# Reordering the queues of a two-layer graph kernel: table steps, gathers, roots and matrix products

## The chip, the cores and the metric

The kernel runs on one core of one Trainium2 chip. The metric is the device time of one execution in microseconds (us). The kernel before has a median of 2475.27 us over three runs (2471.58, 2475.27, 2481.45). A separate execution, taken by the hardware profiler, is the source of every duration below.

The core has five instruction queues: TensorE (PE, matrix products; its weight loads are PEld), VectorE (DVE), ScalarE (ACT), GpSimd (POOL) and SyncE (SP, which here only starts transfers). Each works through its own queue in the order in which the program wrote it, and semaphores hold an instruction until what it needs is done.

## The reference, cut to what matters

```python
# B, C, N = 32, 512, 1024; adj is 512 x 512, all in float32
def layer0(x):
    q, k = einsum('c,bcn->bn', wq, x), einsum('c,bcn->bn', wk, x)
    s = leaky_relu(q[:, None, :] + k[:, :, None], 0.01)
    att = softmax(s, axis=-1)                         # over n, for each m
    agg = einsum('bcn,bmn->bcm', x, att)
    return relu(einsum('oc,bcm->bom', adj, agg) + bm[None, :, None])
def layer1(x):
    return einsum('bnf,nm->bmf', x, adj * adj) + bias
x = layernorm(x + layer0(x))                          # over the last axis, eps 1e-5
x = layernorm(x + layer1(x))
```

## The kernel before, in words

The N x N attention matrix is never made. The score is q[n] + k[m], and leaky ReLU has one slope on each side of zero. So for a given m the softmax over n splits into the n whose q is above -k[m] and those below. With the nodes sorted by q, each side is a prefix or a suffix sum. One batch b goes through these steps:

* `project(b, nt, part)` (L256): four x tiles times [wq, adj^T, wk], giving for each of 8 node tiles (nt) a PSUM tile `zp`, which ACT copies (L264) into `zrow`: q, 512 products, k.
* `peak` (L271) and `spread` (L278 to L302): PE transposes q into every partition (`qb`), and through `mx` (L282) the largest q. DVE takes it as `qmax`, `bw` (L285, L286), saves k as `kc` and overwrites k in `zrow` by 1 (L297, L298). ACT copies `qb` (L293) into `lq`.
* `place` (L315, L319): DVE counts, for each of 8 node tiles, how many q are larger: the ranks. `send` (L324): an indirect DMA, started by POOL, scatters 128 rows of `zrow` to the table `td` in DRAM in rank order. `count` (L343): ACT counts signs of q + k, and `share` (L351 to L361) turns the counts into the rows to gather.
* `fetch` (L371, L376): SP reads the sorted rows back into `zs`, in 9 blocks for the prefix and the suffix.
* `weigh` (L390 to L406): ACT makes exponentials of the sorted q, DVE multiplies them into triangular matrices `lq`.
* `table(b, step)` for step 0 to 8 (L418 to L434): PE multiplies triangles and sorted rows (`tp`), two blocks a step; ACT copies the result (`ts`, L423); the last running sum of each block is carried to the next one, one row by POOL (L427) and one by ACT (L429); SP stores `ts` to `td` in two transfers (L432). Step n+1 on PE needs both carried rows of step n. Step 8 carries none.
* `pick` (L439): an indirect DMA by POOL gathers, for each of 8 node tiles, prefix, suffix and own row (128 rows of 6168 bytes). `shares` (`own` and `norm`, L458 to L472), `scale` (ACT, L485) and `gain` (DVE, L493, two instructions a tile) mix the three rows.
* `turn(b, ot)`: PE transposes the mixture back (`op`, L531), ACT adds bm and applies ReLU (L535). `join`: DVE adds x (L542) and takes mean and variance (`stats`, L502, L504). `root`: POOL computes (variance + eps)^-0.5 (L510, L511). `shift` (DVE, L517) and `apply` (ACT, L523, or DVE, L525) normalise.
* `layer1(b)`: the 1024-wide product with adj * adj, in a Strassen-like form with 7 half-size products (A11, S1, S2, S3, S4, A22, A12; L576, two halves m each) of sums T1 to T4 (`sums`, L559: DVE, or POOL for T2 to T4 with a = 1). DVE reads the products out of PSUM (`read`, L586, 18 reads).
* `stats1`, `shift`, `apply`, `store` normalise the second layer's result `v` and write it out (L622).

The order is written out by hand (`tc.manual_schedule()`): each engine's queue holds its instructions in the order of the calls. The steady part is `slot(s)` for s = 1 to 29, which works on four batches at once: `new` = s+2 is projected, tables are made for `mid` = s+1, batch s goes through gains, turns, joins and layer 1, and `old` = s-1 is normalised and stored. The first part of a slot is a loop of z = 0 to 7 over the projections; from z = 4 on, each z carries two table steps and one turn. A POOL queue of z = 4 therefore reads: roots of `old` 0 and 1, carried row of step 0, carried row of step 1, root of y 0. After the loop come `peak`, the sums T2 to T4 with a = 0, `spread`, and `phase`: table step 8, then the 14 half products with ranks, scatters and gathers threaded between. In it POOL issues the sums T2 to T4 with a = 1, scatters 0 to 2, gathers 0 to 5, scatters 3 and 4, gather 6, scatters 5 to 7, gather 7; SP then starts the fetch of `new`.

`ps_mm` has three PSUM buffers that projections, turns, products and some table steps take in turn, `ps_t` has one, for `qb` and the other table steps. `begin`, `opening` and `end` handle the batches at the two ends, where fewer are in flight.

Of the kernel before, what the change touches and what calls it, by code (L numbers as in the profile page):

```python
# [23 lines left out]
def gat_gcn_resnorm_kernel(  # L24
# [46 lines left out]
    nc = tc.nc  # L71
# [196 lines left out]
    def peak(b):  # L268

        tops[b] = small.tile([P, 1], F32, name=f"q8_{b}", tag="q8")  # L270
        nc.vector.tensor_reduce(tops[b], zrow[:, :, 0], AX.X, ALU.max)  # L271

    def spread(b, to="lq"):
# [13 lines left out]
        if to == "v":  # L287
            qs = vpool.tile([P, N], F32, name=f"qs_{b}", tag="v")
            nc.scalar.copy(qs, qb)
            qb = qs  # L290
        elif to == "lq":
            qs = lq[:, 0:N]
            nc.scalar.copy(qs, qb)  # L293
        else:
            qs = qb
        kc = small.tile([P, NT], F32, name=f"kc_{b}", tag="kc")
        nc.vector.tensor_copy(kc, zrow[:, :, C + 1])  # L297
        nc.vector.memset(zrow[:, :, C + 1], 1.0)  # L298
# [7 lines left out]
        info[b] = (qs, kc, sgn, qmax)  # L306
# [254 lines left out]
    def layer1(b):  # L561
# [10 lines left out]
        def make(w, y, m):  # L572
            if m == 0 or b == B - 1:
                ops[b, w] = ps_mm.tile([P, 2, H], F32, name=f"o{w}_{b}_{m}", tag="mm")
            for a in range(CT // 2):
                nc.tensor.matmul(  # L576
                    ops[b, w][:, m, :], quarters[w][:, a, m * P : (m + 1) * P], part(y, a),
                    start=(a == 0), stop=(a == CT // 2 - 1),
                )
# [9 lines left out]
        for w, y in (  # L589
            ("A11", "Y11"), ("S1", "T1"), ("S2", "T2"), ("S3", "T3"),  # L590
            ("S4", "Y22"), ("A22", "T4"), ("A12", "Y21"),
        ):
            for m in range(2):
                mul.append(lambda w=w, y=y, m=m: make(w, y, m))
        for m in range(2):
            u, v = m, 2 + m
            for name, what in (
# [5 lines left out]
                ("12", (u, hi, "S4", m, u, hi)),  # L603
                ("22", (v, hi, None, m, v, lo)),
                ("21", (v, lo, "A22", m, v, lo)),
                ("11", (u, lo, "A12", m, u, lo)),
# [10 lines left out]
    def stats1(b, mt):  # L617
        stats((1, b, mt), vs[b, mt])
        root(1, b, mt)
# [4 lines left out]
    def rest(b, after):  # L624

        mul, get, reads = layer1(b)
        names = (("c1",), ("c5",), ("u2",), ("u3", "u4"), ("12", "22"), ("21",), ("11",))
        sums(b, ("T1", 0), ("T1", 1), ("T2", 0), ("T3", 0), ("T4", 0))
        for i in range(len(mul)):
            mul[i]()  # L630
            if i == 3:
                sums(b, ("T2", 1), ("T3", 1), ("T4", 1))
            for name in names[i // 2]:
                if b == B - 1:
                    get[name, i % 2]()
                elif i % 2:
                    reads(name)
            after(i)

    def last(b, late):  # L640

        halves = []

        def after(i):
            mt = 1
            if i == 0:
                late(b - 1)
            if i == 11:
                for mt in (2, 3):
                    stats1(b, mt)  # L650
                mt = 1
                st = small.tile([P, NH, 6], F32, name=f"st_1_{b}_{mt}", tag="st")
                nc.vector.bn_stats(st[:, 1, :], vs[b, mt][:, hi])
                halves.append(st)
                for mt in (2, 3):
                    shift(1, b, mt)
                    apply(1, b, mt)
                    store(b, mt)

            if i == 12:  # L660
                stats1(b, 0)
                shift(1, b, 0)
                apply(1, b, 0)
                store(b, 0)

        rest(b, after)
        t, st = vs[b, 1], halves[0]
        nc.vector.bn_stats(st[:, 0, :], t[:, lo])
        mv = small.tile([P, 2], F32, name=f"mv_1_{b}_1", tag="mv")
        nc.vector.bn_aggr(mv, st)  # L670
        due[1, b, 1] = [t, mv]
        root(1, b, 1)
        shift(1, b, 1)
        t, mv, rs, nb = due.pop((1, b, 1))
        nc.scalar.activation(t[:, lo], t[:, lo], AF.Identity, bias=nb, scale=rs)
        nc.vector.tensor_scalar(t[:, hi], t[:, hi], rs, nb, ALU.mult, ALU.add)
        for some in (lo, hi):
            nc.sync.dma_start(out=out[b, P : 2 * P, some], in_=t[:, some])

    def phase(s, mid, new, step=None, done=0):  # L680
# [3 lines left out]
        def rank(*some):  # L684
            for nt in some:
                if nt >= done:
                    place(new, nt)
                    if not done:
                        count(new, nt)
                if nt < 3:  # L690
                    send(new, nt)

        if step is not None:
            table(mid, step, pool=ps_mm)
        mul[0]()
        mul[1]()
        sums(s, ("T2", 1), ("T3", 1), ("T4", 1))
        rank(0, 1, 2)
        mul[2]()
        mul[3]()  # L700
        get["c1", 0]()
        rank(3)
        get["c1", 1]()
        rank(4, 5)
        for mt in range(5):
            pick(mid, mt)
        reads("c5")
        mul[4]()
        mul[5]()
        pick(mid, 5)  # L710
        rank(6)
        get["u2", 0]()
        rank(7)
        get["u2", 1]()
        send(new, 3)
        send(new, 4)
        mul[6]()
        mul[7]()
        pick(mid, 6)
        for nt in range(5, NT):  # L720
            send(new, nt)
        reads("u3", "u4")
        mul[8]()
        mul[9]()
        reads("12", "22")
        mul[10]()
        mul[11]()
        pick(mid, 7)
        fetch(new)
# [4 lines left out]
        scale(mid, range(NT // 2))  # L734
        reads("11")
        gain(mid, range(NT // 2))

    def begin():
# [24 lines left out]
        for z in range(NT):  # L763
# [14 lines left out]
            if z == NT // 2 - 1:  # L778
                fetch(1)
# [3 lines left out]
            if z == NT - 4:  # L783
                weigh(1, 0)
            if z == NT - 3:
                table(1, 0)
                for mt in range(NT):
                    pick(0, mt)
                weigh(1, 1)
            if z == NT - 2:  # L790
                table(1, 1, nc.vector)
        table(1, 2, nc.vector)
        peak(2)
        spread(2, "ps")

    def opening():

        for nt in range(NT // 2):
            place(2, nt)
            table(1, 3 + nt, pool=ps_mm)  # L800
        share(1)
        shares(0, 0, NT // 2)
        scale(0, range(NT // 2))
        count(2, 0)
        table(1, 7, pool=ps_mm)
        count(2, 1)
        gain(0, range(NT // 2))
        shares(0, NT // 2, NT)
        scale(0, range(NT // 2, NT))
        table(1, 8, pool=ps_mm)  # L810
        gain(0, range(NT // 2, NT))
        for nt in range(2, NT):
            count(2, nt)
        for ot in range(CT):
            turn(0, ot)
            join(0, ot)
            root(0, 0, ot)
            load(3, ot)
        shift(0, 0, CT - 1)
        apply(0, 0, CT - 1)  # L820
        sums(0, ("T1", 0), ("T1", 1), ("T2", 0), ("T3", 0), ("T4", 0))
        phase(0, 1, 2, done=NT // 2)

    def slot(s):
# [4 lines left out]
        for z in range(NT):  # L829
# [5 lines left out]
            if step >= 0:  # L835
                table(mid, step)
            if z == NT - 1:
                join(s, CT - 1)
                root(0, s, CT - 1)
# [13 lines left out]
            if z == 3:  # L853
                for mt in (0, 1):
                    stats1(old, mt)
# [6 lines left out]
            if 0 <= ot < CT - 1:  # L862
                join(s, ot)
                root(0, s, ot)
# [5 lines left out]
            if ot == 1:  # L870
                for mt in (2, 3):
                    stats1(old, mt)
# [3 lines left out]
            if new + 1 < B and z >= tz:  # L876
                load(new + 1, ot)
        peak(new)
        shift(0, s, CT - 1)
        sums(s, ("T2", 0), ("T3", 0), ("T4", 0))  # L880
        spread(new)
# [4 lines left out]
        phase(s, mid, new, NB - 1)  # L886

    def end():
# [4 lines left out]
        gain(s, range(NT // 2, NT))  # L893
        weigh(mid, 0)
        for ot in range(CT):
            turn(s, ot)
            table(mid, ot)
            if ot == 1:
                weigh(mid, 1)
            join(s, ot)  # L900
            root(0, s, ot)
            if ot == 1:
                for mt in (0, 1):
                    stats1(old, mt)
            if ot == 2:
                for mt in (0, 1):
                    shift(1, old, mt)
                    apply(1, old, mt, by=nc.vector)
                    store(old, mt)
        shift(0, s, CT - 1)  # L910
        apply(0, s, CT - 1)

        def late(b):
            for mt in (2, 3):
                stats1(b, mt)
            for mt in (2, 3):
                shift(1, b, mt)
                apply(1, b, mt, by=nc.vector)
                store(b, mt)

        def after(i):
            if CT + i < NB:
                table(mid, CT + i)
            if i == 0:
                late(old)
                share(mid)
# [3 lines left out]
            if i in (7, 11):  # L930
                pick(mid, 6 + (i - 7) // 4)

        rest(s, after)
        shares(mid, 0, NT // 2)
        scale(mid, range(NT // 2))
        gain(mid, (0, 1))
        own(mid, NT // 2, NT)
        gain(mid, (2, 3))
        norm(mid, NT // 2, NT)
        scale(mid, range(NT // 2, NT))  # L940
        gain(mid, range(NT // 2, NT))
        for ot in range(CT):
            turn(mid, ot)
            join(mid, ot)
            root(0, mid, ot)
            if ot == 1:
                for mt in (0, 1):
                    stats1(s, mt)
            if ot == 2:
                for mt in (0, 1):  # L950
                    shift(1, s, mt)
                    apply(1, s, mt, by=nc.vector)
                    store(s, mt)
        shift(0, mid, CT - 1)
        apply(0, mid, CT - 1)
        last(mid, late)
# [35 lines left out]
```

## Time and profile before

| | |
|---|---|
| median of three runs | 2475.27 us |
| the profiled execution's own time | 2456.85 us |
| its span, from first to last instruction | 2455.1 us |
| PE busy | 2229.5 us |
| DVE busy | 2005.8 us |
| ACT busy | 1393.3 us |
| POOL busy | 1082.7 us |
| DMA, moved | 548.72 MB, mean 223 GB/s |
| mean granted TensorE clock | 0.965 |
| `qb` of slot 1 to `qb` of slot 29 (28 periods) | 252.68 to 2266.89 us, 71.94 each |
| first product of `phase(0)`, first projection of slot 1 | 172.57, 204.33 us |
| last product of `phase(29)` ends | about 2293.9 us |

The span divides in three: about 204 us of opening, 29 slots, and about 161 us of end. A number such as "[2.03 <-POOL zs L427]" behind an instruction is the idle time of its engine before it, and what released it. Idle time counts only on the engine that sets the pace.

### The profile page before, as it was taken

To read this page: it belongs to the slowest core of one execution; us is meant where nothing else is said; L and a number is where in the kernel's file an instruction comes from. 1 tells how busy PE (TensorE), PEld (TensorE's weight loads), DVE (VectorE), ACT (ScalarE), POOL (GpSimd) and SP (SyncE) were. 2 spreads that over 40 slices of the span, in tenths; PEclk is the share of its full clock that TensorE was granted. 3 is DMA by queue.
4 is the path that set the end of the run, shared out by engine and by line. 5 is a ranking of instruction groups with operands and counts; after the bars stand their busy time and mean duration, and the time that the engine had idled before them with its cause. 6 is when DMAs were issued, how large, how long until landed. Compare 5 with 4: busy or idle time off the path is not lost.

```text
span 2455.1 us, 31484 instructions
## 1 busy us (share of the span) xinstructions
PE 2229.5 (91%) x9520; PEld 1405.4 (57%) x9520; DVE 2005.8 (82%) x4197; ACT 1393.3 (57%) x2176; POOL 1082.7 (44%) x1385
## 2 busy tenths in 40 slices
PE   7858999999999999999999999999999999999665
PEld 6625665566656556655656665565666565566232
DVE  4258888888888888888888888888888888888856
ACT  2553566665556666555666555666655565665521
POOL 1224445444444544444554444455444445543422
PEclk9969999999999999999999999999999999999877
DMA  6546786667777666776766777777677776666631
GB/s 228 152 168 226 232 265 240 218 216 232 255 230 266 238 218 217 235 252 230 259 226 216 226 244 247 238 254 232 208 233 241 240 250 240 220 215 199 225 141 69
DMA packets 176842, 548.72 MB, mean 223 GB/s; under 512 B 26304, under 2 KB 26304, under 8 KB 176672
## 3 DMA queue, kind: packets, MB, share of 16 engines
q1 hardware_dynamic: 117600, 276.65, 38.1%
q0 software_dynamic: 57344, 269.52, 29.1%
q8 instruction: 76, 1.25, 0.2%
q14 instruction: 94, 0.77, 0.1%
q10 hardware_dynamic: 1728, 0.53, 0.1%
HBM read 338.17 MB, written 208.43 MB: 223 GB/s over the span
## 4 chain that ended last, share of the span: by engine, by line
DVE 42%; DMA 15%; PE 13%; issue 8%; POOL 8%; ACT 6%; SPq 0%; DVEq 0%; POOLq 0%; ACTq 0%
DMA rows<-td,idx 13%; DVE st L502 8%; DVE lt L315 8%; DVE v L586 8%; DVE rows L493 7%; PE tp L418 5%; PE zp L256 4%; DVE y L542 3%; POOL rs L511 3%; PE oS L576 2%; DVE rows L559 2%; POOL zs L427 2%; DMA td<-ts 2%; ACT y L535 2%; POOL rs L510 2%
## 5 line engine op out<-in xcount | busy, mean ns | idle before, releaser
L256 PE MATMUL zp<-wmT,x 128*128 128x257 f32 x4096 | 959.4, 387 | 2.9 <-ACT zrow L264 2.9
L256 PEld LDWEIGHTS zp<-wmT,x 128*128 128x128 f32 x4096 | 771.7, 193 | 163.7 <-issue 47.2
L418 PE MATMUL tp<-zs,lq 128*64 128x257 f32 x2304 | 331.9, 406 | 135.3 <-POOL zs L427 118.5
L510 POOL TENSOR_SCALAR rs<-mv 128x1 f32<-128x1 f32 x256 | 74.8, 292 | 759.0 <-DVE mv L504 630.5
L493 DVE SCALAR_TENSOR_TENSOR rows<-rows,ra 128x512 f32<-128x512 f32 x512 | 370.7, 751 | 35.9 <-ACT rows L485 26.8
L423 ACT COPY ts<-tp 128x514 f32<-128x514 f32 x288 | 168.5, 585 | 290.7 <-PE tp L418 249.7
L324 POOL DMA_INDIRECT td<-zrow,ranki x256 | 272.4, 1064 | 119.4 <-DVE ranki L319 54.4
L427 POOL COPY zs<-ts 1x513 f32<-1x513 f32 x254 | 183.5, 722 | 313.2 <-ACT ts L423 313.0
L418 PEld LDWEIGHTS tp<-zs,lq 128*64 128x64 f32 x2304 | 149.6, 140 | 286.2 <-POOL zs L427 168.0
L315 DVE SCALAR_TENSOR_TENSOR lt<-qb,zrow,first 128x1024 int8<-128x1024 f32 x240 | 305.9, 1275 | 1.6
L439 POOL DMA_INDIRECT rows<-td,idx x256 | 263.9, 1031 | 87.3 <-issue 68.7
L461 ACT ACTIVATE ac<-s 128x4 f32<-128x4 f32 x64 | 13.3, 208 | 498.5 <-DVE s L460 498.5
L343 ACT ACTIVATE sg<-lq,kc 128x1024 int8<-128x1024 f32 x232 | 266.3, 1148 | 6.6
L576 PE MATMUL oA<-y,adj_sb 128*128 128x512 f32 x512 | 242.3, 616 | 11.1 <-ACT y L523 11.1
L576 PE MATMUL oS<-rows,ws 128*128 128x512 f32 x512 | 231.7, 604 | 9.7 <-DVE v L586 5.4
L542 DVE TENSOR_TENSOR y<-y,x 128x1024 f32<-128x1024 f32 x128 | 160.8, 1256 | 84.7 <-ACT y L535 84.7
L485 ACT ACTIVATE rows<-rows,ra 128x512 f32<-128x512 f32 x256 | 167.2, 713 | 57.6 <-DVE ra L472 57.6
L264 ACT COPY zrow<-zp 128x514 f32<-128x514 f32 x256 | 147.9, 578 | 89.4 <-PE zp L256 77.7
L531 PE MATMUL op<-ident,rows 128*128 128x128 f32 x1024 | 151.4, 291 | 37.0 <-DVE rows L493 34.3
L511 POOL TENSOR_TENSOR rs<-rs,mhalf 128x1 f32<-128x1 f32 x256 | 172.0, 672 | 21.4
L576 PEld LDWEIGHTS oS<-rows,ws 128*128 128x128 f32 x512 | 97.8, 193 | 138.2 <-issue 128.5
L576 PEld LDWEIGHTS oA<-y,adj_sb 128*128 128x128 f32 x512 | 96.7, 194 | 135.3 <-issue 113.6
(108 smaller groups left out, 2813.3 us busy)
## 6 DMA issues: line engine op xcount, KB each, us to landing
x<-in_x_dram SPq DMA_DIRECT2D x128, 512.0 KB, 4.7
out_dram<-v SPq DMA_DIRECT2D x127, 512.0 KB, 2.7
td<-ts SPq DMA_DIRECT2D x512, 120.5 KB, 2.2
zs<-td SPq DMA_DIRECT2D x64, 602.3 KB, 6.7
zs<-td SPq DMA_DIRECT2D x64, 240.9 KB, 3.3
zs<-td SPq DMA_DIRECT2D x96, 120.5 KB, 3.5
td<-ts SPq DMA_DIRECT2D x64, 96.4 KB, 2.0
td<-zs SPq DMA_DIRECT2D x8, 514.0 KB, 9.1
```

Of the source, the lines that this page charges most:

```text
L256: nc.tensor.matmul(zp[:, h, 0:CE], xb[ct][:, nt * P : (nt + 1) * P], wmT[:, ct, h * CE : (h + 1) * CE], start=(ct == 0), stop=(ct == CT - 1),)
L315: nc.vector.scalar_tensor_tensor(lt, qs, zrow[:, nt, 0:1], first[:, o : o + N], ALU.subtract, ALU.is_lt, accum_out=rank[:, nt : nt + 1],)
L324: sc = nc.gpsimd.indirect_dma_start(out=td[:, :], out_offset=bass.IndirectOffsetOnAxis(ap=ranki[:, nt : nt + 1], axis=0), in_=zrow[:, nt, ...
L343: nc.scalar.activation(sg, qs, AF.Sign, bias=kc[:, nt : nt + 1], accum_out=sgn[:, nt : nt + 1])
L418: nc.tensor.matmul(tp[i * G : (i + 1) * G, h, 0:CE], lw[:, ks[i], :], zs[:, j, h * CE : (h + 1) * CE], start=True, stop=True,)
L427: by.tensor_copy(zs[0:1, to, 1:ZW], ts[0:1, 1:ZW])
L439: nc.gpsimd.indirect_dma_start(out=rows[:, mt, :], out_offset=None, in_=tds[b].rearrange("(s u) c -> s (u c)", u=3), in_offset=bass.Indire ...
L493: nc.vector.scalar_tensor_tensor(u, g[:, k, i, 1 : C + 1], ra[:, k, i : i + 1], u, ALU.mult, ALU.add)
L502: nc.vector.bn_stats(st[:, h, :], t[:, h * H : (h + 1) * H])
L511: nc.gpsimd.tensor_tensor(rs, rs, mhalf, ALU.pow)
L542: nc.vector.tensor_tensor(t, t, xs[b][ot], ALU.add)
L576: nc.tensor.matmul(ops[b, w][:, m, :], quarters[w][:, a, m * P : (m + 1) * P], part(y, a), start=(a == 0), stop=(a == CT // 2 - 1),)
```

## The change

* `peak` now also saves `kc` and writes the ones; before, `spread` did. `spread` always copies `qb` to `lq` (or to `v`).
* In `slot`: root of y 0, 1 and 2 moves from behind its `join` to behind the first table step of the next z; the roots of `old` follow the first table step of z = 4 and z = 6 (`roots`, split from `stats1`). The root of y 3 comes after the loop, behind the carried row of step 7. After the loop the order is `peak`, `spread`, table step 8, and then the normalisations of y 3 and of `old` 2 and 3; before, it was the sums, `spread`, the normalisations, and step 8.
* In `phase`: the sums T2 to T4 with a = 0 (DVE) move in between the ranks. POOL issues two sums, gathers 0 and 1, the third sum, then scatter 0, gather 2, scatter 1, gather 3, scatter 2, gathers 4 and 5, scatter 3, gather 6, scatters 4 and 5, gather 7, scatters 6 and 7. A22 comes before S4, with the reads in the order 22, 21, 12, 11; the gains of tiles 0 and 1 stand before the reads of A12.
* `begin` makes no table of batch 1, and issues the gathers of batch 0 earlier; `opening` makes the 9 table steps of batch 1 between the gains, turns and joins of batch 0, and `phase(0)` is now the same as all others.
* `end`: steps 0 and 1 of the last table stand between gains; T1 is taken before the last join; the old batch's normalisation is applied by ACT in `rest`; the last batch's v 0 and v 1 are normalised and stored by halves.

The diff, cut to its core:

```diff
 def peak(b):
     nc.vector.tensor_reduce(tops[b], zrow[:, :, 0], AX.X, ALU.max)
+    nc.vector.tensor_copy(kc, zrow[:, :, C + 1])
+    nc.vector.memset(zrow[:, :, C + 1], 1.0)
...
 def make(w, y, m):
-    if m == 0 or b == B - 1:
+    if m == 0 or b == B - 1 and w in ("S4", "A12"):
...
-            ("S4", "Y22"), ("A22", "T4"), ("A12", "Y21"),
+            ("A22", "T4"), ("S4", "Y22"), ("A12", "Y21"),
...
+    def ready(b, *some):
+        for mt in some:
+            shift(1, b, mt)
+        for mt in some:
+            apply(1, b, mt)
+            store(b, mt)
...
 def rest(b, after):
-    names = (("c1",), ("c5",), ("u2",), ("u3", "u4"), ("12", "22"), ("21",), ("11",))
-    sums(b, ("T1", 0), ("T1", 1), ("T2", 0), ("T3", 0), ("T4", 0))
+    names = (("c1",), ("c5",), ("u2",), ("u3", "u4", "22"), ("21",), ("12",), ("11",))
     for i in range(len(mul)):
         mul[i]()
-        if i == 3:
-            sums(b, ("T2", 1), ("T3", 1), ("T4", 1))
+        if i == 0:
+            sums(b, ("T2", 0), ("T2", 1), ("T3", 1), ("T3", 0), ("T4", 1), ("T4", 0))
...
 def phase(s, mid, new):
     mul[0]()
     mul[1]()
-    sums(s, ("T2", 1), ("T3", 1), ("T4", 1))
-    rank(0, 1, 2)
+    rank(0, 1)
+    sums(s, ("T2", 0), ("T2", 1), ("T3", 1))
+    pick(mid, 0)
+    pick(mid, 1)
     mul[2]()
     mul[3]()
+    rank(2)
+    sums(s, ("T3", 0), ("T4", 1))
     get["c1", 0]()
+    for nt in range(3):
+        send(new, nt)
+        pick(mid, nt + 2)
     rank(3)
...
+    pick(mid, 7)
+    send(new, 6)
+    send(new, 7)
+    fetch(new)
+    reads("u3", "u4", "22")
     mul[10]()
     mul[11]()
-    pick(mid, 7)
-    fetch(new)
     reads("21")
     mul[12]()
     mul[13]()
     shares(mid, 0, NT // 2)
     scale(mid, range(NT // 2))
+    reads("12")
+    gain(mid, (0, 1))
     reads("11")
-    gain(mid, range(NT // 2))
+    gain(mid, (2, 3))
...
 def opening():
-    for nt in range(NT // 2):
-        place(2, nt)
-        table(1, 3 + nt, pool=ps_mm)
...
+    gain(0, range(NT // 2))
+    weigh(1, 0)
+    table(1, 0)
+    shares(0, NT // 2, NT)
+    scale(0, range(NT // 2, NT))
+    table(1, 1)
+    gain(0, (4, 5))
+    weigh(1, 1)
+    table(1, 2)
+    gain(0, (6, 7))
     for ot in range(CT):
         turn(0, ot)
+        table(1, 3 + ot)
         join(0, ot)
         root(0, 0, ot)
         load(3, ot)
+    table(1, NB - 2, pool=ps_mm)
+    spread(2)
+    table(1, NB - 1, pool=ps_mm)
...
 def slot(s):
             if step >= 0:
                 table(mid, step)
+            if ot == 0:
+                roots(old, 0, 1)
+            if ot > 0:
+                root(0, s, ot - 1)
+            if ot == 2:
+                roots(old, 2, 3)
             if z == NT - 1:
                 join(s, CT - 1)
-                root(0, s, CT - 1)
...
                 join(s, ot)
-                root(0, s, ot)
...
+        root(0, s, CT - 1)
         peak(new)
+        spread(new)
+        table(mid, NB - 1, pool=ps_mm)
         shift(0, s, CT - 1)
-        sums(s, ("T2", 0), ("T3", 0), ("T4", 0))
-        spread(new)
         apply(0, s, CT - 1)
         for mt in (2, 3):
             apply(1, old, mt)
             store(old, mt)
-        phase(s, mid, new, NB - 1)
+        phase(s, mid, new)
...
 def end():
+        weigh(mid, 0)
+        table(mid, 0)
+        gain(s, (6,))
+        table(mid, 1)
+        gain(s, (7,))
+        weigh(mid, 1)
         for ot in range(CT):
             turn(s, ot)
+            if ot == CT - 1:
+                sums(s, ("T1", 0), ("T1", 1))
+            table(mid, 2 + ot)
             join(s, ot)
...
```

## The prediction, written before the changed kernel was run

> **What bounds the kernel now.** I read the busy table first, then the stretch of 28 equal slots, then what PE waited for in it, then one slot in order of time on PE and on POOL.
>
> ```profile
> PE 2229.5 (91%) x9520; PEld 1405.4 (57%) x9520; DVE 2005.8 (82%) x4197; ACT 1393.3 (57%) x2176; POOL 1082.7 (44%) x1385
> PEclk9969999999999999999999999999999999999877
> ```
> ```profile
> 252.68:2266.89 2014.21, 1915.25 (x8319) 1214.36 (x8317) 1737.71 (x3642) 1220.93 (x1904) 943.39 (x1204) 0.99 0.71 235
> ```
> ```profile
> PE tp L418 <- POOL zs L427: 87.8, 111, 2.0
> PE tp L418 <- DVE lq L398: 10.5, 12, 1.6
> ```
>
> Columns of the middle row: stretch, length, busy PE, PEld, DVE, ACT, POOL, clock, DMA share, GB/s. PE is busy 1915.25 of 2014.21 us. The 99 us left are two waits: for the carried row that POOL copies (87.8 us) and for the triangles from DVE (10.5). So a slot of 71.94 us holds 3.5 us of PE idle time, and that is the most that reordering can win there, the clock apart. One slot on PE:
>
> ```profile
> 1085.17 1.29 PE L418 MATMUL tp<-zs,lq 128*64 128x257 f32 x8 [1.59 <-DVE lq L398]
> 1091.25 1.09 PE L418 MATMUL tp<-zs,lq 128*64 128x257 f32 x8 [2.03 <-POOL zs L427]
> ...
> 1105.04 1.09 PE L418 MATMUL tp<-zs,lq 128*64 128x257 f32 x8 [0.23 <-POOL zs L427]
> ...
> 1112.23 1.09 PE L418 MATMUL tp<-zs,lq 128*64 128x257 f32 x8 [0.39 <-POOL zs L427]
> 1113.25 1.09 PE L278 MATMUL qb<-ident,zrow 128*128 128x128 f32 x8
> 1114.17 0.27 PE L282 MATMUL mx<-ident,q 128*128 128x128 f32 x1
> 1114.92 1.09 PE L418 MATMUL tp<-zs,lq 128*64 128x257 f32 x8 [0.47 <-POOL zs L427]
> ```
>
> The four waits on POOL stand before steps 1, 5, 7 and 8, and come back in nearly every slot. What POOL did before step 1 and before step 7 (another slot):
>
> ```profile
> 1234.45 0.21 POOL L510 TENSOR_SCALAR rs<-mv 128x1 f32<-128x1 f32 x1 [0.58 <-DVE mv L504]
> 1234.75 0.57 POOL L511 TENSOR_TENSOR rs<-rs,mhalf 128x1 f32<-128x1 f32 x1
> 1235.28 0.60 POOL L427 COPY zs<-ts 1x513 f32<-1x513 f32 x1
> ...
> 1256.97 1.52 POOL L427 COPY zs<-ts 1x513 f32<-1x513 f32 x1 [0.28 <-ACT ts L423]
> ```
>
> The roots of the old batch stood in the queue ahead of the carried row and waited for DVE's statistics; ACT had `ts` ready at 1231.76. The second copy took 1.52 instead of 0.60 us beside DVE's y addition (1256.80 to 1258.03).
>
> The clock: from each step 1, four microseconds; the last figures are clock, DMA, GB/s.
>
> ```profile
> 372.83:376.83 4.00, 4.00 (x14) 2.52 (x15) 3.89 (x8) 1.20 (x2) 1.16 (x3) 0.57 0.11 33
> 445.50:449.50 4.00, 4.00 (x25) 2.43 (x25) 3.89 (x8) 1.20 (x2) 1.16 (x3) 1.00 0.21 62
> ```
>
> In 12 of 28 slots the clock falls to 0.57 to 0.69 after the 2.03 us gap, and step 1 to step 5 then takes 15.42 instead of 13.79 us: 1.63 us, or 0.70 a slot on average.
>
> **What the Trainium skill says.** "TensorE: Matmul & The Clock Gate", Part 1: PE runs at half clock after an idle window of about 3.4 us. Here 2.03 us, with sparse work around it, is enough in 12 of 28 slots. "SBUF — State Buffer", Who interferes with whom: a DVE instruction with two SBUF inputs and a GpSimd instruction that reads SBUF block each other, the first to issue wins. The copy of 1.52 us agrees. "DMA: Bandwidth & Descriptors", Anatomy of one DMA: 2.0 us plus bytes at 436 GB/s; a gather (0.79 MB) would take 3.8 us. The trace has a median of 8.3 to landing, so gathers queue behind each other; between 1208 and 1218 us the DMA moved 386 to 428 GB/s at a share of about 1.
>
> **Part 1, roots behind the carried rows (each slot).** Step 1: the row is ready 1.4 us after step 0 ends (0.59 copy, 0.60 row, hand-overs), and PE has 2.85 us of turn and projection in between. Wait 2.03 becomes 0. The two roots (0.87 each) end about 5.3 us after step 0 starts, before row 1 can start (5.85), so nothing queues behind them. Step 5: 0.23 becomes 0.
>
> Step 7 and 8: here a new chain arises. The root of y 2 now stands behind the row of step 6, and `join` of y 3 begins with the shift that needs this root. From the start of step 6: `ts` starts at 1.15; copy and hand-over 0.65; row 0.62; root 0.87; then shift, y addition, statistics and `peak`, which took 2.90 from 1256.72 to 1259.62; with the hand-overs 6.3. `mx`, in order on PE, can't start before, and step 8 follows 0.3 later: 6.7 after step 6. Before, `mx` started 5.35 and step 8 6.10 after step 6. So this end loses 0.6, although step 7 loses its wait (the y addition no longer meets the copy) and root 3 no longer precedes row 7. Net: 2.03 + 0.23 - 0.6 = 1.66.
>
> **Part 2, gathers, scatters and DVE order (each slot).** Step 8's `ts` is copied right after the `lq` copy, ahead of three applies of 1.24, so gather 0 can start some 3.5 us earlier after step 6 (12.6 instead of 16.1). From there POOL issues 16 DMAs and one sum, 1.3 us each: gather 7 starts at 30.9 (before 32.3), scatter 7 at 33.5 (before, the last scatter 31.1). The bytes, 8.4 MB at about 0.40 MB/us, need 21 us, and both orders are limited by that: I take the last scatter to land at 38 to 39, the fetch starting there as before (38.2). PE wants the first triangles at 47.9, and fetch to triangles took 9.1 (1220.72 to about 1229.8): about 0.8 of slack. Gather 7, 2 to 4 us earlier, takes the late `shares` off that path; DVE's queue (8 ranks of 1.39, 3 sums, 18 reads of 0.62, gains of 0.73) runs unbroken to 39.4 and reaches the triangles at 47. The wait of 0.38 a slot becomes about 0.1: gain 0.3. Bounds: 0.38, or a loss if the fetch is late (rival C and E). Product order: S4 waits for the reads of S2, done 0.6 before; A22 for those of S1, 1.1 before; cost nothing, covered by these margins, else their shortfall. Two reads before and two after gains 0 and 1: the third projection needs them 2.5 later; nothing.
>
> Normalisations delayed behind step 8 push ACT's counts by 1 us; ACT is idle for 10 us after them (1203.4 to 1213.4). SP's two stores of step 8 now precede the two output stores; nobody waits for the latter.
>
> **Clock.** The 2.03 gap goes, but a gap of 1.1 to 1.4 at `mx` appears; whether that trips the clock no trace shows. Bounds per slot: gain 0.70, or loss of 0.3 (every slot tripped costs 1.63, against 0.70 now, less what remains); I take half, 0.35.
>
> Sum per slot: 1.66 + 0.3 + 0.35 = 2.3; 29 slots 67. Slot 1 alone also had a 2.59 wait for `zrow` and a late triangle: 3. Together 70.
>
> **Part 3, opening.** Before, phase(0) started at 172.57 and took 31.8 us. After: projections of batch 2 end at 118 (103.97 plus four of 3.52); gathers 0 to 3 land about 120, sharing the DMA with the fetch; shares and four gains to 128.5; step 0 there; steps 1, 2 and four gains to 143; four turns with steps 3 to 6 and joins of 3 to 3.9 us each, steps 7, 8, `mx` to 163. Then a phase of 24.3 as in every slot: slot 1 starts at 187 instead of 204.3. Gain 17 (8 to 25; DVE and the cold clock decide).
>
> **Part 4, end.** From the last product of phase(29): the last batch but one starts its products at 35 before, 34 now (more table steps first); finishes them at 74.9 before, 66 now (three steps instead of five inside, but step 7 waits 4 us for its row behind three POOL sums); the last turn can start at 96.4 before, 85 now; the end comes 64.8 later before, about 56 now (old statistics no longer precede S1). Gain 20 (10 to 30).
>
> **Sum.** 70 + 17 + 20 = 107, made against the profiled execution: 2456.85 - 107 = 2350. The median shown is 18 us above it; carried over in proportion, 2475.27 x 2350/2456.85 = 2367.
>
> **Rivals.**
> A, the forecast, 58%: 2342 to 2392.
> B, 17%: the chain to `mx` is hidden or shorter and the clock stays full: 3.5 + 0.7 a slot, 122 + 3 + 17 + 20 = 162: 2313. For: all PE waits of a slot lie in the moved rows. Against: the queue order of root 2.
> C, 12%: scatters behind gathers make the fetch 2.3 us late, 1.5 past the slack: 29 x 0.8 + 40 = 63: 2412. For: scatters 6 and 7 start last and the DMA share is 1.
> D, 5%: gains and new waits cancel, or the reordering acts only at the two ends and they overrun: about 2475.
> E, slower, 8%: the same place, the fetch gating the triangles, but decisive: if the DMA moves the 8.4 MB at 0.30 instead of 0.40 MB/us once gathers and scatters alternate with the output stores, it takes 28 instead of 21 us. Each microsecond past the slack costs 29. The gain is used up at 107/29 + 0.8 = 4.5 us late; at 5.2 the time is 2495. Against: the queue already ran near 400 GB/s with both kinds mixed.
>
> **How the numbers follow.** The range 2310 to 2425 takes in A, most of B and C, leaving D, E and tails, under 2 in 10. About 0.5% (12 us) is what a measurement can tell from no change. Faster by more: A, B, C, 87%; within: 5%; slower: 8%.
>
> **What would show it.** Right: no idle before step 1; an idle of over 1 us before `mx`, released by DVE's peak; slot period near 69.6; triangles waited for under 0.2 a slot; first product of phase(0) near 163. Wrong: PE waiting for triangles by 1 us or more with SP's fetch released late by the scatters (C, E); no gap at `mx` (B); a clock below 0.7 after `mx` in most slots.

## The result, and the profile after

Over 20 runs each, the changed kernel takes 2464.72 us (2459.72 to 2473.41) and the kernel before 2475.47 us (2464.1 to 2485.0). The ratio is 0.9969, 95% interval [0.9955, 0.9983]: a gain of 0.3%, some 11 us, where 108 us were forecast, and outside the forecast range.

One caution for the two traces. The profiled execution of the kernel before (2456.85 us) lies below all its 20 timed runs, that of the changed kernel (2473.41 us) is the longest of its 20. Side by side the traces make the change look slower by 17 us; set against the medians that is 27 us, about 1 us a slot, too much. So I read the traces for which waits are there, and leave the sums to the timed runs.

The three stretches of the profiled executions. The columns are stretch, length, busy PE, PEld, DVE, ACT, POOL, clock, DMA share and GB/s; the rows are the 28 steady slots, all before them, all after them.

```profile
242.17:2282.37 2040.20, 1927.36 (x8318) 1220.92 (x8316) 1729.34 (x3641) 1217.59 (x1905) 955.93 (x1204) 0.99 0.72 232
0.00:242.17 242.17, 192.34 (x884) 138.63 (x884) 130.82 (x288) 111.64 (x186) 77.05 (x99) 0.92 0.62 200
2282.37:2471.60 189.23, 114.12 (x323) 52.42 (x321) 129.57 (x261) 71.56 (x96) 63.80 (x84) 0.79 0.41 142
```

The opening is 10.5 us shorter (252.68 before). The end is as long as before (188.21). The slots hold no gain: 72.86 us each, in this long execution. By size, the 11 us of the timed runs are what the opening won. What PE waited for in the slots of the changed kernel (total, times, longest):

```profile
PE tp L417 <- POOL zs L426: 62.9, 40, 3.8
PE mx L286 <- DVE q L271: 18.5, 28, 0.7
PE tp L417 <- DVE lq L397: 15.9, 21, 2.0
PE qb L282 <- ACT zrow L264: 10.0, 28, 0.4
```

The carried row still heads the list. But it is another row, as one slot on PE shows:

```profile
1094.84 1.36 PE L417 MATMUL tp<-zs,lq 128*64 128x257 f32 x8 [0.55 <-DVE lq L397]
...
1098.90 1.09 PE L417 MATMUL tp<-zs,lq 128*64 128x257 f32 x8
...
1102.41 1.16 PE L417 MATMUL tp<-zs,lq 128*64 128x257 f32 x8 [0.48 <-POOL zs L426]
...
1109.22 1.09 PE L417 MATMUL tp<-zs,lq 128*64 128x257 f32 x8
...
1114.59 1.09 PE L417 MATMUL tp<-zs,lq 128*64 128x257 f32 x8 [1.52 <-POOL zs L426]
...
1122.35 0.98 PE L282 MATMUL qb<-ident,zrow 128*128 128x128 f32 x7
1123.72 0.32 PE L282 MATMUL qb<-ident,zrow 128*128 128x128 f32 x1 [0.39 <-ACT zrow L264]
1124.71 0.32 PE L286 MATMUL mx<-ident,q 128*128 128x128 f32 x1 [0.66 <-DVE q L271]
```

Step 1 (1098.90) starts without a wait: the 2.03 us gap is gone, as forecast. Step 5 (1114.59) now waits 1.52 us; over the slots this wait was 1.4 to 3.8 us, 56.6 us in 27 slots, where it was 0.23 before. Follow it back. POOL copied that row as soon as `ts` was there; ACT was late with `ts` of step 4:

```profile
1108.71 1.24 ACT L522 ACTIVATE y<-y,nb,rs 128x1024 f32<-128x1024 f32 x1
1113.28 0.59 ACT L422 COPY ts<-tp 128x514 f32<-128x514 f32 x1 [3.33 <-DMA td<-ts]
1113.90 0.61 ACT L428 COPY zs<-ts 1x513 f32<-1x513 f32 x1
```

ACT stood idle for 3.33 us until a store of `ts` had landed. `ts` comes from `tpool`, which has two buffers: step 4 takes the buffer of step 2, so it waits until the stores of step 2 are in DRAM. On SP's queue those stood behind two output stores and an input load:

```profile
1106.11 1.28 SPq L633 DMA_DIRECT2D out_dram<-v x2
1107.43 0.44 SPq L162 DMA_DIRECT2D x<-in_x_dram  x1
1107.97 2.37 SPq L431 DMA_DIRECT2D td<-ts  x4
```

Each of the three DMAs ahead carries 512 KB. The output stores wait until DVE has normalised `v`, and the stores of step 2, whose `ts` was ready at 1104.24, wait behind them. ACT's wait for these stores in the slots (total, times, longest), before and after:

```profile
ACT ts L423 <- DMA td<-ts: 11.0, 9, 1.8
```
```profile
ACT ts L422 <- DMA td<-ts: 104.1, 27, 5.6
```

Counted from step 0 of its slot, the buffer comes free after 17.4 us before (the landing) and 18.4 us after (ACT's copy, which waits for it), in the median: about as late in both. Before, PE was so late by its gap at step 1 that it hardly met this; now it comes to step 4 some 2 us earlier (14.0 us after step 0 instead of 15.8) and waits at step 5. The old stall had covered the next one.

### The profile page after: what moved, and what is told of

Read it like the earlier page. It is cut to its first block, busy times and chain, and to the rows that moved or that the text cites. A ratio compares the mean times of both kernels' runs of the same rounds, so it can differ in the third digit from the quotient of the medians.

```text
span 2471.6 us, 31266 instructions
## 1 busy us (share of the span) xinstructions
PE 2233.8 (90%) x9520; PEld 1412.0 (57%) x9520; DVE 1989.7 (81%) x4188; ACT 1400.8 (57%) x2185; POOL 1096.8 (44%) x1387
## 3 DMA queue, kind: packets, MB, share of 16 engines
q1 hardware_dynamic: 117744, 276.65, 37.4%
## 5 line engine op out<-in xcount | busy, mean ns | idle before, releaser
L426 POOL COPY zs<-ts 1x513 f32<-1x513 f32 x256 | 164.2, 641 | 945.1 <-ACT ts L422 945.1
L417 PEld LDWEIGHTS tp<-zs,lq 128*64 128x64 f32 x2304 | 157.2, 140 | 282.3 <-POOL zs L426 136.1
L438 POOL DMA_INDIRECT rows<-td,idx x256 | 280.1, 1094 | 82.5 <-issue 63.0
L342 ACT ACTIVATE sg<-lq,kc 128x1024 int8<-128x1024 f32 x240 | 275.1, 1146 | 6.8
L522 ACT ACTIVATE y<-y,nb,rs 128x1024 f32<-128x1024 f32 x128 | 158.4, 1238 | 48.2 <-DVE nb L516 46.5
L516 DVE SCALAR_TENSOR_TENSOR nb<-mv,rs 128x1 f32<-128x1 f32 x256 | 35.9, 150 | 164.9 <-POOL rs L510 160.6
L501 DVE BATCH_NORM_STATS2 st<-y 128x6 f32<-128x512 f32 x256 | 164.7, 685 | 4.4
L530 PE MATMUL op<-ident,rows 128*128 128x128 f32 x1024 | 152.1, 295 | 17.7 <-DVE rows L492 17.7
```

The costliest lines, as they stand in the source:

```text
L342: nc.scalar.activation(sg, qs, AF.Sign, bias=kc[:, nt : nt + 1], accum_out=sgn[:, nt : nt + 1])
L417: nc.tensor.matmul(tp[i * G : (i + 1) * G, h, 0:CE], lw[:, ks[i], :], zs[:, j, h * CE : (h + 1) * CE], start=True, stop=True,)
L438: nc.gpsimd.indirect_dma_start(out=rows[:, mt, :], out_offset=None, in_=tds[b].rearrange("(s u) c -> s (u c)", u=3), in_offset=bass.Indire ...
L501: nc.vector.bn_stats(st[:, h, :], t[:, h * H : (h + 1) * H])
```

## The experiments

Each run is given as a ratio to the kernel before on the same chip, with its 95% interval; the chips differ (the kernel before took 2458 to 2471 us on them). Slot periods and waits are from each run's own trace, over its 28 steady slots.

**e1, a third staging buffer.** Room came from small tiles of short life, which get two buffers instead of three.

```diff
-    tpool = ctx.enter_context(tc.tile_pool(name="tpool", bufs=2))
+    tpool = ctx.enter_context(tc.tile_pool(name="tpool", bufs=3))
-    small = ctx.enter_context(tc.tile_pool(name="small", bufs=3))
+    small = ctx.enter_context(tc.tile_pool(name="small", bufs=2))
...
+        st = small.tile([P, NH, 6], F32, name=f"st_{who}", tag="st", bufs=3)
```

(`kc`, `mv`, `rs` and `nb` keep three, as `st` does.)

> The changed kernel with three table staging buffers instead of two (room is made by giving the small tiles of short life two buffers instead of three; nothing else moves). Theory T: the gap before step 1 was not won but handed on; step 4's copy out of PSUM waits until the stores of step 2 have landed, because both staging buffers are taken, and step 5 then waits for its carried row. With a third buffer ACT's wait for these stores (104 us in the 28 slots) falls below 10, PE's wait before step 5 (56 us) below 8, and the half-clock stretches behind it go: 56 + about 19 us, so 2385 to 2410 us. Rival R: the row is late for another reason (POOL's or ACT's queue, or DVE), and the buffer only shows where the wait is taken: 2450 to 2475 us, with PE's wait before step 5 still over 40 us.

Measured: 2405.47 us, ratio 0.9737 [0.9698, 0.9776]; slot 70.52 us. ACT's wait for the stores is down from 104.1 to 8.7 us, step 5 does not wait, and PE's list in the slots reads

```profile
PE mx L286 <- DVE q L271: 18.5, 28, 0.7
PE tp L417 <- DVE lq L397: 17.5, 22, 1.8
PE tp L417 <- POOL zs L426: 11.1, 25, 1.5
```

T holds. The 11.1 us left for POOL are step 2 and step 7, not step 5. The small tiles lost a buffer in the same edit; e2 leaves them as they were.

**e2, two buffers, but the output stores further back on SP's queue.**

```diff
                     apply(1, old, mt, by=nc.vector)
-                    store(old, mt)
+            if ot in (1, 2):
+                store(old, ot - 1)
```

> The changed kernel with two buffers, but the output stores of the old batch's first two tiles stand one behind the stores of step 3 and one behind those of step 5 in SP's queue, instead of both ahead of the stores of step 2. Theory T with its cause in SP's queue (1 MB of output stores, which wait for DVE's normalisation, ahead of the stores that free the buffer): the stores of step 2 are issued at about 8.5 us after step 0 instead of 12.5, ACT's wait for them falls below 20 us in the 28 slots, time 2390 to 2415 us. Rival S: not the order on the queue but the DMA's traffic or the landing itself is slow: the wait stays above 60 us, time 2445 to 2470 us.

Measured: 2400.45 us, 0.9711 [0.9665, 0.9758]; slot 70.39 us. The stores of step 2 leave 9.2 us after step 0 instead of 12.8 (medians). ACT does not wait for them, and step 5 does not wait; all that is left of PE's waits for POOL in the slots is

```profile
PE tp L417 <- POOL zs L426: 9.6, 21, 1.4
```

So the order on SP's queue, with two buffers, was the cause, and either remedy takes it away.

**e3, the root of y 2 back ahead of step 6's row.**

```diff
             project(new, z, 0)
+            if z == NT - 1:
+                root(0, s, ot - 1)
             if step >= 0:
                 table(mid, step)
...
-            if ot > 0:
+            if 0 < ot < CT - 1:
                 root(0, s, ot - 1)
```

> The changed kernel with only the root of y 2 put back ahead of step 6, so ahead of its carried row on POOL. Theory M (as predicted): this root behind the row delays the last join and with it the copy of the last zrow, the peak and mx: the two idle stretches at the end of the table (0.36 and 0.66 us a slot) go, step 8 then waits some 0.4 us for the row of step 7 as in the kernel before. Gain 0.6 to 0.9 us a slot, 17 to 25 us: 2440 to 2448 us. Rival: the root placed earlier waits for its statistics and holds up the row of step 6, so step 7 waits instead: no gain or up to 10 us slower, 2462 to 2475 us.

Measured: 2437.37 us, 0.9879 [0.9838, 0.992], 0.9% below the changed kernel's ratio, or 22 us. PE's wait for the last `zrow` is gone and that for `mx` falls from 18.5 to 3.8 us; step 5 still waits (54 us). M holds: 17 to 25 us were expected.

**e4, both.**

> Both: three staging buffers and the root of y 2 ahead of step 6. If T and M are right and independent, the gains add: 75 + 20 us, 2360 to 2390 us, slot period near 69.3 us. If the slot has a third limit close behind (the triangles from DVE at step 0, or the next landing), the sum falls short: 2390 to 2420 us, with the new wait named in the trace.

Measured: 2387.79 us, 0.9667 [0.9629, 0.9705]; slot 69.86 us. On the same chip it is 17.7 us below e1. By the ratios, the buffer alone takes 57 us off the changed kernel, the root alone 22, both 75: they nearly add up.

**e5, e6, e7: a square on the kernel before.** e5 adds the third buffer to it, e6 moves its roots alone, e7 does both. The edit for the roots in `slot` (the statistics then go without their root):

```diff
             if step >= 0:
                 table(mid, step)
+            if ot == 0:
+                root(1, old, 0)
+                root(1, old, 1)
+            if ot > 0:
+                root(0, s, ot - 1)
+            if ot == 2:
+                root(1, old, 2)
+                root(1, old, 3)
...
             if 0 <= ot < CT - 1:
                 join(s, ot)
-                root(0, s, ot)
```

> The kernel before with the third table staging buffer alone. Theory T: in the kernel before the two buffers were a limit just behind the gap at step 1 (ACT waited 11 us for them in the 28 slots, 9 times), so the buffer alone is worth 0 to 10 us: 2460 to 2475 us. Rival: the buffers were a bound of their own already, and most of what the third buffer brought to the changed kernel (60 us) comes here too: 2410 to 2430 us.

> The kernel before with the roots alone moved behind the carried rows in a slot, as in the changed kernel; phase, step 8, gathers, opening and end stay. Theory T: the 2.03 us wait at step 1 goes in every slot and comes back, larger or smaller, at step 5 behind ACT's wait for the stores of step 2; with the 0.9 us at the end of the table the slot is as long as before or up to 1 us longer: 2465 to 2500 us. The prediction's own step (2.03 + 0.23 - 0.6 a slot won): 2425 us.

> The kernel before with both: the roots moved and the third staging buffer. Theory T: now the moved roots are worth what was forecast for them, 1.7 us a slot and the clock's 0.35 to 0.7: 58 to 67 us, 2408 to 2418 us. If the gain of the third buffer on the changed kernel came from its other order of gathers and scatters, this one stays above 2440 us.

Measured on one chip, where the kernel before took 2457.94 us:

| | two buffers | three buffers |
|---|---|---|
| roots ahead of the rows | 1 (before) | 0.9984 [0.9971, 0.9996] |
| roots behind the rows | 0.9993 [0.9979, 1.0007] | 0.9736 [0.972, 0.9752] |

Alone, the buffer is worth 0.2% and the move of the roots nothing that can be told; together they take 2.6%, 65 us. e6 shows the exchange in the plainest form. Its PE waits and its ACT wait for the stores:

```profile
PE tp L418 <- POOL zs L427: 47.0, 27, 3.1
```
```profile
ACT ts L423 <- DMA td<-ts: 88.0, 25, 4.9
```

In e7 both are nearly gone:

```profile
PE tp L418 <- POOL zs L427: 0.5, 2, 0.3
```
```profile
ACT ts L423 <- DMA td<-ts: 1.9, 2, 0.9
```

Its slots are

```profile
246.21:2200.85 1954.64, 1907.67 (x8319) 1201.87 (x8317) 1704.16 (x3641) 1216.91 (x1905) 941.63 (x1204) 1.00 0.74 242
```

That is 69.81 us each, 2.13 less than in the trace of the kernel before. e7 has none of the change's other parts (gathers, step 8, opening, end) and is as short as e1, which has them all: 0.9736 against 0.9737, though on two chips.

**e8, the end.** On e4, the old batches' statistics, roots, normalisations and stores go between the last turns instead of between the products; the same is done for the last batch.

```diff
             join(s, ot)
             root(0, s, ot)
+            if ot in (0, 2):
+                stats1(old, ot, ot + 1)
+                roots(old, ot, ot + 1)
+            if ot == 1:
+                ready(old, 0, 1)
         shift(0, s, CT - 1)
         apply(0, s, CT - 1)
+        ready(old, 2, 3)
```

> The kernel of e4 (three staging buffers, root of y 2 ahead of step 6) with the old batches' statistics, roots, normalisations and stores of the end put between the last batches' turns, ahead of their products, instead of between the products. Theory V: the end won nothing because DVE's first reads of the products wait for output stores that free the four v buffers (3.2 + 0.5 and 2.9 + 0.5 us for the last batch but one, the same again for the last), and PE then waits for DVE; with the stores done earlier these waits go: from the last steady slot to the end 8 to 14 us less than the 189 us of the changed kernel, 2374 to 2381 us. Rival: DVE's joins are delayed by the statistics between them (2.9 us each pair) as in the kernel before, and the gain is lost there: within 4 us of e4, 2384 to 2392 us.

Measured: 2371.00 us, 0.9655 [0.9624, 0.9685]. The ratio can't be told from e4's on another chip; the trace can. From the last slot's `qb` to the end took 189.2 us in e4 and 180.3 in e8; it takes 188 to 191 us in all nine traces without this edit and 178 to 183 in all five with it. DVE's waits in the end, the changed kernel first, then e8:

```profile
DVE v L585 <- DMA out_dram<-v: 14.3, 8, 3.2
```
```profile
DVE v L585 <- DMA out_dram<-v: 2.6, 2, 2.1
```

V holds as far as it goes: `vpool` has four buffers, the first read of a new batch's products waits until the old batch's tile has landed in DRAM, and most of this wait is gone. But the edit moves DVE's statistics together with the stores, so how much of the 8.9 us is due to the stores alone was not tried.

**e9, gather 7 last.** On e8, `pick(mid, 7)` goes behind `send(new, 6)` and `send(new, 7)`.

> The kernel of e8 with gather 7 issued behind scatters 6 and 7 instead of ahead of them. Theory F: in the changed order the last scatter is issued later, the fetch of the next table goes with it (some 6.7 us later), and its late landing, not DVE's queue, holds the triangles: ACT waits 2.5 us for it in every slot. With the last scatter 1.3 us earlier the fetch leaves 1.3 us earlier, ACT's wait falls to about 1.2 us and DVE's idle time before the triangles from 1.3 to about 0; PE's wait at step 0 (17.5 us in 28 slots) falls below 8: 10 to 17 us less than e8. Rival: the bytes on the DMA set the landing, whatever the order (as the prediction had it): the fetch stays within 0.3 us of where it was, nothing changes (within 4 us of e8).

Measured: 2369.92 us, 0.9587 [0.9564, 0.9609]; slot 69.63 us against 69.68 in e8. The two ratios differ more than the slots, but they come from two chips (before: 2470.46 and 2457.94 us). e10 and e11 below differ by the same edit on one chip, and there it is worth 3.5 us. From `qb` the fetch left after 33.9 us instead of 36.5, and the wait of ACT's first exponential for it, 2.5 us a slot, went to zero. So the sum of the bytes, the same in both orders, does not set the landing. Of the 2.6 us, 1.5 are the earlier issue of the last scatter; in the other 1.1 it landed sooner after its issue (5.6 instead of 6.7 us), with gather 7's 0.79 MB no longer ahead of it. But next to nothing was won. What DVE waited for most in e8, then in e9:

```profile
DVE lq L397 <- ACT w L389: 70.7, 56, 2.5
```
```profile
DVE s L457 <- DMA rows<-td,idx: 62.4, 28, 3.0
```

Now the second `shares` waits for gather 7, 2.2 us in every slot. POOL has 16 DMAs to issue, about 1.3 us each; whichever comes last, DVE waits for it. PE's wait for the triangles rose from 17.5 to 29.6 us. F was right that the issue moves the fetch, and wrong on the price: 10 to 17 us were expected.

**e10, e11, e12.** e10 is e8 with an instruction on POOL in the opening that reads gather 3's output ahead of gathers 4 to 7. e11 is e9 with it. e12 is e11 with scatter 0 ahead of the sums; the rest of the order stays.

```diff
-                for mt in range(NT):
+                for mt in range(NT // 2):
                     pick(0, mt)
+                hold = small.tile([P, 1], F32, name="hold", tag="rs", bufs=3)
+                nc.gpsimd.tensor_scalar(
+                    hold, rows[:, NT // 2 - 1, 0:1], EPS, None, ALU.add
+                )
+                for mt in range(NT // 2, NT):
+                    pick(0, mt)
```

> The kernel of e8 with one small POOL instruction in the opening that reads what gather 3 wrote, so that gathers 4 to 7 are issued only when the first four have landed. Theory O: the opening missed because the first four gathers shared the DMA with the other four and the fetch and landed at 128 to 130 us instead of the forecast 120; apart they land near 122, DVE's first shares and step 0 come 5 to 7 us earlier (step 0 from 137 to about 131), and the first product of phase(0) comes 3 to 6 us earlier (171 to 166). Rival: the gathers are limited by their own rate of packets, four take as long as before: shares still near 128 and the second four later, so the opening is up to 5 us longer.

> Both edits on the kernel of e8. If both theories hold the gains add: 14 to 22 us less than e8, a ratio to the kernel before of 0.957 to 0.960.

> As e11, with scatter 0 issued as soon as its ranks are there, ahead of the three sums on POOL, and gather 2 ahead of scatter 1. Theory F: once DVE's queue holds the triangles again, an earlier scatter brings little: within 6 us of e11. If the fetch still gates after e11, 1 us more a slot is won: 20 us or more less than e11.

Measured: 2374.10 us, 0.9604 [0.9582, 0.9626]; 2370.61 us, 0.9596 [0.9573, 0.9619]; 2376.49 us, 0.9618 [0.9595, 0.964]. None beats e9. e11's ratio lies in the expected 0.957 to 0.960, but its time is only 0.4 us below e8's, where 14 to 22 were expected. O falls: apart from the others the first four gathers were as slow. POOL in e10:

```profile
114.64 0.99 POOL L438 DMA_INDIRECT rows<-td,idx  x1 [0.30 <-issue]
129.26 0.23 POOL L791 TENSOR_SCALAR hold<-rows 128x1 f32<-128x1 f32 x1 [13.62 <-DMA rows<-td,idx]
```

The four were in at 129.3 us; in e8, with all eight in flight, DVE had them at 128.5. The DMA was full meanwhile (share 0.97 to 1.03 from 114 to 130 us) and moved 225 to 324 GB/s. e12 has the earliest fetch (32.7 us after `qb`), and there PE waits for DVE's reads of the products (25 us in the slots); it is 5.9 us slower than e11, within the 6 us expected.

## Why the prediction was wrong, step by step

**Part 1, the roots.** The gain of the step itself was sized rightly. It said 1.66 us a slot plus 0.35 for the clock; e7, which has just this step and a free buffer, won 2.13 by the traces, and its 65 us are 2.2 a slot. In the traces the 2.13 are 1.86 of PE's waits and 0.27 of its busy time. The chain to `mx` was right too: `mx` starts 6.3 us after step 6 (1118.38 to 1124.71; forecast 6.3) and step 8 0.3 later; undoing it (e3) gives 22 us. The step that failed is "Step 5: 0.23 becomes 0". I asked what is late next for the roots on POOL and for `mx`, but not for the staging buffers. With PE 2 us earlier at step 4, the buffer of step 2 was not free: 2.03 us at step 1 became, in the trace, 2.0 at step 5. The margin could have been read from the profile before: ACT's wait for `td<-ts` stood there with 11.0 us in 9 slots, a margin of nothing. The Trainium skill, "DMA: Bandwidth & Descriptors", Anatomy of one DMA, gives 2.0 us plus the bytes at 436 GB/s for a transfer that GpSimd starts. Taken for these, which SyncE starts, it is a rough estimate: three times 0.52 MB ahead is 3.6 us, the two stores of step 2 (0.25 MB) 2.0 plus 0.6, together 6.2; the trace has 5.3 from their issue (1107.97) to ACT's copy (1113.28).

**The clock.** I took half the possible gain for want of evidence on the gap at `mx`. That gap did not trip it: the granted clock at step 8 was 1.00 in all 28 slots. The new one at step 5 did, in 8 of 28 slots, and step 5 to step 6 took 5.2 to 6.7 us there instead of 3.8, 16 us in all. In the runs without that wait the mean clock of the slots is 1.00.

**Part 2, gathers and scatters.** Forecast: the wait for the triangles goes from 0.38 to 0.1 us a slot, as both orders are limited by bytes. Measured: 0.57, and 0.22 more before step 2, whose row waits behind ACT's late exponentials. The failing term is "I take the last scatter to land at 38 to 39": the fetch left 41.4 us after step 6 (37.4 after `qb`). The last scatter was issued at 34.6 (forecast 33.5, before 31.1), and the fetch left 6.7 us after that, where the forecast left some 5 and the kernel before took 7.1; e9 shows that the order does move the landing. Rival C had named this place, at 0.8 us a slot; it was about 0.4. e1 against e7 bounds the whole of the change's other slot parts: 70.52 against 69.81, a loss of 0.7 us a slot where 0.3 was to be won. Of the 20 us in 28 slots, 8 are triangles, 11 are rows, 4 are longer busy PE time, and 7 the other way are e7's waits before products, which the change's order of products and reads avoids; the rest I can't place.

**Part 3, the opening.** Forecast 17 us, measured 10.5 to slot 1's `qb`, in which the 3 us forecast for slot 1 are included. The phase took 24.5 us, as forecast (24.3). The failing term is "gathers 0 to 3 land about 120":

```profile
130.40 0.16 DVE L457 TENSOR_TENSOR s<-rows,kc 128x4 f32<-128x4 f32 x1 [6.25 <-DMA rows<-td,idx]
```

These 10 us appear unchanged at step 0 (138.97, forecast 128.5) and at phase(0) (173.09, forecast 163). e10 shows that it is not the four other gathers. The bytes point to the rate and to the fetch, which ran beside them: from the first gather's issue (111.50) to these shares the DMA moved 5.37 MB, at 284 GB/s. The four gathers alone are 3.2 MB; landing by 120 would have taken 370 GB/s for them and nothing for the fetch. No run keeps the fetch apart.

**Part 4, the end.** Forecast 20 us, measured none. From the last product of phase(29): the products start at 35.0 (forecast 34), finish at 74.0 (66), the first tile of the last turns is transposed at 95.6 (85), and the rest takes 65.3 (56); before, these two were 95.7 and 65.3. "Old statistics no longer precede S1" was counted as a gain, without the `v` buffers that these statistics free: DVE's reads waited 14.3 us for output stores, in two lots of 7. e8 takes most of that wait away, and its last part measures 59.3 where e4, from which it was made, has 64.5. Up to the last product e8 won 3.0 us on e4 (74.7 against 77.7): with the statistics between the joins its products start 2.0 later and then run 5.0 shorter. Of the 10.6 us missing at the last turns 8 are there at the last product. The 39.0 us of products are 32.2 of busy PE, 4.3 for the row of step 7 and 2.5 for DVE before A22: the forecast's 32 us were no more than the busy time and had no room for the 4 us of step 7 that the same sentence names. The other 2.6 us lie between the last product and the turns, where DVE waits 5.4 us for gathered rows.

**Rivals and signs.** Of the signs of being right, the one at step 1 came true and the idle before `mx` in part (0.4 us before `qb` ends and 0.7 before `mx`); the slot period, the triangles and phase(0) did not. No sign of being wrong named step 5. No rival gave the mechanism. D had the outcome, "gains and new waits cancel", for 5%; it lacked a place. B's reason, that all PE waits lie in the moved rows, was true of the trace and not enough: a wait list shows who came last, not who came second.

## What to carry to other kernels

When a stall of 2 us is taken out, look for the resource that would have been late by 2 us less: for every engine that now runs earlier, find the buffer it writes next, who frees it, and what stands ahead of that on its queue. A small entry in the wait list of an engine off the critical path (here ACT, 11 us in 9 slots) is such a margin, already used up. Large stores that wait for a computation don't belong ahead of small stores that free a buffer (e2); with the third buffer, the root of y 2, the stores at the end and gather 7 last (e9) the kernel came to 0.9587 [0.9564, 0.9609], over ten times the change's own gain.

## What the hardware showed that I had not expected

The clock. The gaps before step 5 make a scale of their own: at 1.4 to 1.7 us the granted clock stayed at 1.00, of five gaps between 1.88 and 2.21 us one brought it down, from 2.42 us up all seven did. Four microseconds from step 5 after a gap of 3.71 us and after one of 1.52 (the last columns are clock, DMA share, GB/s):

```profile
670.80:674.80 4.00, 4.00 (x17) 2.86 (x18) 3.00 (x8) 3.42 (x7) 3.36 (x7) 0.50 0.31 94
1114.60:1118.60 4.00, 4.00 (x26) 2.94 (x28) 3.00 (x8) 3.94 (x7) 3.36 (x7) 1.00 0.46 126
```

The Trainium skill, "TensorE: Matmul & The Clock Gate", Part 1, puts the idle window at about 3.4 us; here gaps from 1.88 us up lowered the clock, and in the kernel before one of 2.03 us did so in 12 of 28 slots.

The DMA. With a share of 1.0 it moved about 310 GB/s where gathers and the fetch ran together in the opening, and four gathers took as long to land with four more behind them as without: 18.2 us from the first issue to the shares in e8, 18.6 to the reading instruction in e10. The prediction had read 386 to 428 GB/s at such a share in a slot.
